# A matrix attention kernel: four products of two units take their operand blocks in reverse order

## The chip, the core and the metric

The kernel runs on one NeuronCore of a Trainium2 chip. The metric is the device time of one execution in microseconds (us). Before the change it was run five times: median 2456.31 us, from 2454.04 to 2456.42.

## What is computed

For each of four images x (64 x 64 positions, 256 channels), three projections are made, then an attention over the N = 4096 positions of the flattened image, then a scaled residual:

```python
q = jnp.einsum('bwhc,cd->bwhd', x, Wq) + bq
k = jnp.einsum('bwhc,cd->bwhd', x, Wk) + bk
v = jnp.einsum('bwhc,cd->bwhd', x, Wv) + bv
pq = q.reshape(B, -1, N)
pk = k.reshape(B, -1, N)
pv = v.reshape(B, -1, N)
energy = jnp.einsum('bcn,bcm->bnm', pq, pk)
attention = jax.nn.softmax(energy, axis=-1)
out = jnp.einsum('bcm,bnm->bcn', pv, attention)
return gamma * out + x
```

pq and pk have 128 rows (channels), pv has 256. The softmax runs over m, the 4096 positions of k and v.

## The kernel before, in words

**Stages.** The images follow each other. For each, sixteen projection steps (lines 493 to 505) transpose x and make q, k and v; then 128 steps, `for u in range(STEPS)` (line 507), do the attention. A *group* g is 256 of the 4096 columns n; there are 16 groups. A group is worked through in eight *units* t = 0 to 7, `g, t = divmod(u, NU)`; a unit is 512 of the 4096 positions m, in four blocks of 128.

**Precision.** The matmuls of the attention are of type fp32r. Each operand is held as an upper part h, a remainder l, and a form d that mixes both with a small factor E; three products put the result together: h with `vh`, l with `vl` (both added up in `acc`), and d with `vd` (added up in `bb`). The three forms of v lie in SBUF for the whole image: `vh` and `vl` have rows of VC = 260 floats (256 channels, a column of ones for the softmax's sum, and padding; lines 220 and 221), `vd` rows of 256 floats (line 222). The h, l and d of a unit are tiles of 4 x 256 floats in rotating buffers (three for h, two each for l and d).

**One step u.** It issues, in this order: the energies of unit u + 3 in two halves (`energy`, lines 317 to 339; six matmuls each, of 256 columns, into `sa` and `sb`, with an exponential of each on ACT); between the halves, the product x*y on DVE and the upper part h on ACT for unit u + 2 (`join`, line 344, `upper`, line 349); a load of the k tile for unit u + 5 (line 314, on POOL's queue); l and d of unit u + 1 on DVE (`halves`, lines 355 and 358); and the products of unit u (`attend`, line 380). When a group ends, its result is copied out of PSUM and finished during the first steps of the next group (`finish`, lines 400 to 422); this puts four transposes (line 417) on PE, behind the products of t = 1. In the first group of an image there are none. In the last three steps of an image there are no more energies. On PE, then, behind the products of a unit t stand the energies that the next step issues.

**The order on PE** is written out by hand (`tc.manual_schedule()`): no scheduler moves it. In `attend` there are 24 matmuls for a unit: for h, then l, then d; in each for j = 0, 1 (the two halves of 128 columns n, `NJ` = 2), and in each of these over i = 0 to 3, the four blocks of m. The block number is 2t, 2t + 16, 2t + 1, 2t + 17 for i = 0, 1, 2, 3. The weights of a product are a block of 128 x 128 of h, l or d; the moving operand is a row block of vh, vl (258 columns) or vd (256 columns). All four products of one (form, j) add up in the same place of PSUM. Line 378 has the block number, line 377 the loop over i, and line 382 the addresses' step, `left[:, i, j * P : (j + 1) * P]`.

Of the kernel before, what the change touches and what calls it, by code (L numbers as in the profile page):

```python
# [20 lines left out]
def kernel(  # L21
# [154 lines left out]
    NJ = NB // P  # L176
# [24 lines left out]
    with ExitStack() as fast:  # L201
# [161 lines left out]
        def attend(b, u):  # L363

            g, t = divmod(u, NU)
            if t == 0:
                now["acc"] = [
                    ps_o.tile([P, C + 2], F32, tag=f"a{j}", name=f"a{j}_{b}_{g}")
                    for j in range(NJ)
                ]  # L370
                now["bb"] = ps_o.tile([P, NJ, C], F32, tag="bb", name=f"bb_{b}_{g}")
            h, l, d = units[b, u]
            acc, bb = now["acc"], now["bb"]
            for left, right in ((h, vh), (l, vl), (d, vd)):
                for j in range(NJ):
                    out_ = bb[:, j, :] if left is d else acc[j]
                    for i in range(4):
                        m = 2 * t + i // 2 + NI * (i % 2)

                        nc.tensor.matmul(  # L380
                            out_,
                            left[:, i, j * P : (j + 1) * P],
                            right[:, m, : out_.shape[1]],
                            start=(t == i == 0 and (left is h or left is d and j == 0)),
                            stop=(t == NU - 1 and i == 3 and left is not h),
                            skip_group_check=True,
                        )
            if t == NU - 1 and (b, g) != (B - 1, NG - 1):
                o = now["o"] = work.tile([P, NJ, C + 2], F32, tag="o", name=f"o_{b}_{g}")
                for j in range(NJ):  # L390
                    nc.scalar.activation(o[:, j, :], acc[j], AF.Identity, scale=1.0 + E)
# [94 lines left out]
        for b in range(B):  # L486
# [20 lines left out]
            for u in range(STEPS):  # L507
                g, t = divmod(u, NU)
# [33 lines left out]
                for forms in beside:  # L542
                    next(forms)
                attend(b, u)
                if (b, u) == (B - 1, STEPS - 1):
                    finish_last(b, g, loads.pop((b, "x", g)))
# [11 lines left out]
    NJ = NB // P  # L558
# [131 lines left out]
```

## Time and profile before

One profiled execution took 2456.11 us as a run; the span from its first to its last instruction was 2454.3 us.

| what | value |
|---|---|
| median of five runs | 2456.31 us |
| profiled execution / its span | 2456.11 / 2454.3 us |
| mean granted TensorE clock | 0.998 |
| h products (line 380), 4096 matmuls of 258 columns | 574.4 us busy |
| l products, 4096 of 258 columns | 572.8 us busy |
| d products, 4096 of 256 columns | 558.6 us busy |
| energies (line 330), 4096 into sa, 2048 into sb | 735.6 and 567.0 us busy |
| longest wait of another engine for PE: POOL for sb before a load of k | 1547.1 us in 428 waits |
| DMA, mean | 203 GB/s |

How to read it: "PE" is the matmuls, "PEld" the loading of their weights, which runs beside them. A matmul's duration in a row (279 to 283 ns) is not the time between two of them: they are pipelined, and the end of each is modelled. The time that a stretch of matmuls takes is read from starts: the start of the first matmul behind the stretch minus the start of its first. Consecutive matmuls of the same line and tiles stand in one row of the timeline, with their number (x8).

Lines 199 and 124 in a row of PE are the warm-up transposes and the transposes of x at the start; line 460 is the last output's transposes at the end.

### The profile page before, as it was taken

To read this page: it belongs to the slowest core of one execution; us is meant where nothing else is said; L and a number is where in the kernel's file an instruction comes from. 1 tells how busy PE (TensorE), PEld (TensorE's weight loads), DVE (VectorE), ACT (ScalarE), POOL (GpSimd) and SP (SyncE) were. 2 spreads that over 40 slices of the span, in tenths; PEclk is the share of its full clock that TensorE was granted. 3 is DMA by queue.
4 is the path that set the end of the run, shared out by engine and by line. 5 is a ranking of instruction groups with operands and counts; after the bars stand their busy time and mean duration, and the time that the engine had idled before them with its cause. 6 is when DMAs were issued, how large, how long until landed. Compare 5 with 4: busy or idle time off the path is not lost.

```text
span 2454.3 us, 50024 instructions
## 1 busy us (share of the span) xinstructions
PE 2440.5 (99%) x19982; PEld 2409.2 (98%) x19982; DVE 2099.6 (86%) x2314; ACT 1796.9 (73%) x3201; POOL 425.8 (17%) x781
## 2 busy tenths in 40 slices
PE   9999999999999999999999999999999999999998
PEld 8999999999899999999989999999998999999998
DVE  5988888888698888888869888888886988888887
ACT  5877777777677777777667777777766777777775
POOL 4211111111411111111141111111114111111110
PEclk9999999999999999999999999999999999999999
DMA  7666666665776666666477666666647766666663
GB/s 230 214 209 203 209 206 199 209 207 159 226 224 200 206 211 203 205 201 207 150 240 224 200 201 210 203 208 202 205 142 245 228 203 198 207 205 212 202 202 112
DMA packets 137407, 498.92 MB, mean 203 GB/s; under 512 B 15536, under 2 KB 57264, under 8 KB 137168
## 3 DMA queue, kind: packets, MB, share of 16 engines
q0 software_dynamic: 92320, 453.17, 60.1%
q1 hardware_dynamic: 44304, 42.22, 5.6%
q8 instruction: 160, 2.62, 0.4%
q14 instruction: 79, 0.65, 0.1%
q10 hardware_dynamic: 544, 0.26, 0.0%
HBM read 445.25 MB, written 50.33 MB: 202 GB/s over the span
## 4 chain that ended last, share of the span: by engine, by line


## 5 line engine op out<-in xcount | busy, mean ns | idle before, releaser
L334 ACT ACTIVATE x<-sa 128x512 f32<-128x512 f32 x1024 | 613.7, 599 | 514.2 <-PE sa L330 512.0
L344 DVE TENSOR_TENSOR x<-x,y 128x1024 f32<-128x1024 f32 x512 | 626.9, 1224 | 233.9 <-ACT y L334 233.9
L330 PE MATMUL sa<-q,k 128*128 128x256 f32 x4096 | 735.6, 279 | 0.0
L355 DVE TENSOR_TENSOR l<-x,h 128x1024 fp32r<-128x1024 f32 x512 | 623.9, 1219 | 0.0
L358 DVE SCALAR_TENSOR_TENSOR d<-h,x 128x1024 fp32r<-128x1024 f32 x512 | 623.8, 1218 | 0.0
L330 PEld LDWEIGHTS sa<-q,k 128*128 128x128 f32 x4096 | 619.5, 188 | 0.5
L334 ACT ACTIVATE y<-sb 128x512 f32<-128x512 f32 x1024 | 615.2, 601 | 0.0
L380 PE MATMUL a<-vh,h 128*128 128x258 f32 x4096 | 574.4, 283 | 0.0
L380 PE MATMUL a<-vl,l 128*128 128x258 f32 x4096 | 572.8, 282 | 0.0
L330 PE MATMUL sb<-q,k 128*128 128x256 f32 x2048 | 567.0, 277 | 0.0
L380 PE MATMUL bb<-vd,d 128*128 128x256 f32 x4096 | 558.6, 279 | 0.0
L314 POOL DMA_DIRECT2D k<-kf x512 | 280.0, 547 | 1572.1 <-PE sb L330 1547.1
L349 ACT ACTIVATE h<-x 128x1024 fp32r<-128x1024 f32 x512 | 543.7, 1062 | 8.4 <-DVE x L344 7.9
L380 PEld LDWEIGHTS a<-vl,l 128*128 128x128 f32 x4096 | 525.3, 189 | 0.0
L380 PEld LDWEIGHTS a<-vh,h 128*128 128x128 f32 x4096 | 522.9, 189 | 0.0
L380 PEld LDWEIGHTS bb<-vd,d 128*128 128x128 f32 x4096 | 515.1, 188 | 0.0
L330 PEld LDWEIGHTS sb<-q,k 128*128 128x128 f32 x2048 | 384.5, 188 | 0.2 <-DVE q L266 0.2
L137 PE MATMUL qk<-wqk_sb,xts 128*128 128x256 f32 x512 | 122.4, 382 | 0.0
L158 PE MATMUL v<-xts,wv_sb 128*128 128x256 f32 x512 | 120.3, 379 | 0.0
L158 PEld LDWEIGHTS v<-xts,wv_sb 128*128 128x128 f32 x512 | 97.3, 190 | 13.2
L137 PEld LDWEIGHTS qk<-wqk_sb,xts 128*128 128x128 f32 x512 | 93.0, 191 | 10.3
L275 POOL DMA_DIRECT2D qd<-qks x128 | 69.4, 550 | 180.7 <-DVE qks L146 171.7
(56 smaller groups left out, 866.0 us busy)
## 6 DMA issues: line engine op xcount, KB each, us to landing
k<-kf POOLq DMA_DIRECT2D x512, 768.0 KB, 4.7
x<-in_x_dram SPq DMA_DIRECT2D x128, 256.0 KB, 3.9
kf<-f POOLq DMA_DIRECT2D x64, 384.0 KB, 3.9
out_dram<-x POOLq DMA_DIRECT2D x63, 256.0 KB, 2.6
qd<-qks POOLq DMA_DIRECT2D x128, 64.0 KB, 3.0
qr<-qd SPq DMA_DIRECT2D x64, 128.0 KB, 3.6
wv_sb<-in_L_conv_Wv_dram POOLq DMA_DIRECT2D x1, 256.0 KB, 7.3
out_dram<-x SPq DMA_DIRECT2D x1, 256.0 KB, 4.1
```

The lines of the kernel that those rows point to most:

```text
L137: nc.tensor.matmul(qk[:, s, :], self.xt[i][:, k, s, :], wqk_sb[:, k, :], start=(k == 0), stop=(k == KC - 1),)
L158: nc.tensor.matmul(vp[:, eh, :], wv_sb[:, k, eh * P : (eh + 1) * P], self.xt[i][:, k].rearrange("p s a -> p (s a)"), start=(k == 0), stop= ...
L275: nc.gpsimd.dma_start(qd[b, i // 2 + NG // 2 * s][:, i % 2, :], x[:, s, :C2])
L314: nc.gpsimd.dma_start(t.rearrange("p (i s) f d -> p i s (f d)", s=2), kf[b, u % NU])
L330: nc.tensor.matmul(to[:, i], kt[:, 2 * k + i, f, :], q[:, f], start=first, stop=last)
L334: nc.scalar.activation(to[:, 2 * k : 2 * k + 2, :], sp.rearrange("p i j d -> p i (j d)"), AF.Exp, scale=scale,)
L344: nc.vector.tensor_tensor(x, x, y, ALU.mult)
L349: nc.scalar.activation(h, units[b, u], AF.Identity, scale=UPPER)
L355: nc.vector.tensor_tensor(l, x, h.bitcast(F32), ALU.subtract)
L358: nc.vector.scalar_tensor_tensor(d, h.bitcast(F32), 1.0 + E, x, ALU.mult, ALU.subtract)
L380: nc.tensor.matmul(out_, left[:, i, j * P : (j + 1) * P], right[:, m, : out_.shape[1]], start=(t == i == 0 and (left is h or left is d and ...
```

## The change

In the units t = 1 and t = 3 of each group, the four l products for j = 1, the last four l products of the unit, run over i = 3, 2, 1, 0 in place of 0, 1, 2, 3. So the block numbers there are 2t + 17, 2t + 1, 2t + 16, 2t. All other products keep their order; each product keeps its own weights, its own rows of vl and its place in PSUM.

```diff
             for left, right in ((h, vh), (l, vl), (d, vd)):
                 for j in range(NJ):
                     out_ = bb[:, j, :] if left is d else acc[j]
-                    for i in range(4):
+                    back = left is l and j == NJ - 1 and t in (1, 3)
+                    for i in reversed(range(4)) if back else range(4):
                         m = 2 * t + i // 2 + NI * (i % 2)
```

The changed file has three more lines than the file before, so line 380 of before is line 383 of after.

## The prediction

> **What bounds the kernel now.** I read the page first (busy shares, clock), then PE's waits, then the groups by form, then the timeline of PE alone over one group, and last the start of every single matmul in the trace.
>
> ```profile
> span 2454.3 us, 50024 instructions
> PE 2440.5 (99%) x19982; PEld 2409.2 (98%) x19982; DVE 2099.6 (86%) x2314; ACT 1796.9 (73%) x3201; POOL 425.8 (17%) x781
> PEclk9999999999999999999999999999999999999999
> ```
>
> PE is busy from end to end at a granted clock of 0.998. Its own waits are three rows of 5.6 us in all, at the start and the very end:
>
> ```profile
> PE wp L199 <- POOL ident masks.py:199: 2.4, 1, 2.4
> PE xt L124 <- DMA x<-in_x_dram: 2.1, 1, 2.1
> PE ot L460 <- DVE o L455: 1.1, 1, 1.1
> ```
>
> So in between, the time is the number of matmuls times the pace at which they start, and nothing on DVE, ACT, POOL or the queues sets it. The pace is not one number. The timeline of PE for t=2 to t=4 of one group (start, length, engine, line; what counts is the start of the next row minus that of a row; the length has the modelled tail of the last matmul in it):
>
> ```profile
> 865.08 1.12 PE L380 MATMUL a<-vh,h 128*128 128x258 f32 x8
> 866.03 1.12 PE L380 MATMUL a<-vl,l 128*128 128x258 f32 x8
> 866.99 1.08 PE L380 MATMUL bb<-vd,d 128*128 128x256 f32 x8
> 867.90 0.39 PE L330 MATMUL sa<-q,k 128*128 128x256 f32 x2
> ...
> 869.26 1.11 PE L380 MATMUL a<-vh,h 128*128 128x258 f32 x8
> 870.21 1.12 PE L380 MATMUL a<-vl,l 128*128 128x258 f32 x8
> 871.17 1.11 PE L380 MATMUL bb<-vd,d 128*128 128x256 f32 x8
> 872.12 0.40 PE L330 MATMUL sa<-q,k 128*128 128x256 f32 x2
> ...
> 873.54 1.12 PE L380 MATMUL a<-vh,h 128*128 128x258 f32 x8
> 874.49 1.12 PE L380 MATMUL a<-vl,l 128*128 128x258 f32 x8
> 875.45 1.09 PE L380 MATMUL bb<-vd,d 128*128 128x256 f32 x8
> 876.38 0.39 PE L330 MATMUL sa<-q,k 128*128 128x256 f32 x2
> ```
>
> The eight d products take 0.91 us in t=2 and 0.95 in t=3; the twelve energy matmuls behind them (next h start minus first sa start) take 1.36 and 1.42. Same instructions, same forms, no wait. By single starts, the d products and energies settle at one of two paces: 113.3 ns (**short**), or a cycle of 117.5, 117.5 and 118.3 ns, mean 117.8 (**long**). Six of the eight units of a group (t=0, 2, 4, 5, 6, 7) settle short and two, t=1 and t=3, settle long; this repeats within a nanosecond in the groups of all four images. The h and l products never settle: they wander between 113 and 125 ns.
>
> The pace has a memory: in t=1 the transposes of the previous group's output come behind the d products, and the energies behind these run short again. In the first group of an image there are no such transposes, and the energies of t=1 stay long:
>
> ```profile
> 83.50 1.10 PE L380 MATMUL bb<-vd,d 128*128 128x256 f32 x8
> 84.44 0.40 PE L330 MATMUL sa<-q,k 128*128 128x256 f32 x2
> ...
> 85.85 1.12 PE L380 MATMUL a<-vh,h 128*128 128x258 f32 x8
> ```
>
> 85.85 minus 84.44 is 1.41. The pace also depends on addresses: rows of vh and vl are 260 floats, 1040 bytes, so each step of m moves the moving operand by 16 bytes against its weights (whose steps are 512), while vd's rows are 1024 bytes and keep one place. In t=1 all rounds of four but the first repeat 120.0, 120.9, 123.3, 115.8 ns over i, for h and for l. So: the last l products leave the PE's two reads in some relation, and the d products, all with one relation of addresses, fall from it into short or long and carry it through the energies until h begins.
>
> **The change, part by part.** The built program differs from before in the operands of 512 matmuls (4 images x 16 groups x 2 units x 4) and nowhere else: counts, waits and semaphore updates stand at the same places; l of a unit is read by the same eight matmuls and released by the last of them. No engine gets more or other work, and no queue is passed. What is left is pace.
>
> *Reordered products.* The four take 480.0 ns (t=1) and 475.9 (t=3) now. The same four in the other six units take 468 to 483, mean 476. Reversed they lie, by the nearest rows, between 12 ns less and 7 more; I take 476: 4 ns off in t=1, nothing in t=3, 64 x 4 = 0.3 us (ends: 1.3 off, 0.6 on).
>
> *d products of t=3.* 948 ns now; the six short units take 916 to 930, mean 923. If released, 25 ns off (18 to 32). *Energies of t=3:* 12 x (117.8 - 113.3) = 54 ns off. Together 79 (72 to 86), and all 64 groups have energies there: 64 x 79 = 5.1 us (4.6 to 5.5).
>
> *d products of t=1.* 944 ns, the last of them slowed by the transpose behind it; released, 923 plus 4 for that: 17 off (10 to 24), in 60 groups 1.0 us. In the four first groups the energies are long too: 4 x (19 + 54) = 0.3 us. Together 1.3 (0.9 to 1.7).
>
> *t=4 behind a short t=3.* It now starts from long energies, then from short ones. The nearest row is t=2, seen both ways: h, l and d take 2831 ns from long (first group), 2826 from short. 64 x 5 = 0.3 us off; with 8 ns to either side, from 0.2 on to 0.8 off.
>
> *Cover.* A unit of t=3 shortens from 4.28 us to about 4.20, which is what t=4 takes with the same work beside it: DVE's three passes of 1.2 us, ACT's exponentials (which wait for PE). k tiles land 4.7 us after issue and are loaded two units, over 8 us, ahead. l for t=4 is ready at 870.19 and first read at 874.49. Nothing is late next.
>
> Is the new entry short? The trace does not show it. By the row of v last read before d, t=0 to 7 end on m = 17, 19, 21, 23, 25, 27, 29, 31; 19 and 23 give long. The change ends on m=2 and m=6: even rows, which never come last now. The bounds are no release (0) and full release; I take release, since six of eight entries end short, from very different pasts, and t=2 ends short from both kinds of entry.
>
> [...]
>
> **The sum.** 5.1 + 1.3 + 0.3 + 0.3 = 7.0 us off. The profiled execution took 2456.11 us (its span 2454.3 and 1.8 around it) and would take 2449.1; the median of the runs is 2456.31, so 2449.3 us.
>
> **The rivals.** 0.2% is 4.9 us, about what a measurement of this kernel can tell from no change.
>
> - *Only t=3 is released:* 5.1 + 0.3 from t=4: 2450.9 us. For it: the two units enter from different rows (m=2, m=6), so they need not go together.
> - *Only t=1:* 1.3 + 0.3: 2454.7 us.
> [...]
> - *Slower: the long pace spreads.* t=3 stays long, leaves its energies in another place of the three-step cycle, and t=4 (short today, always entered from t=3's long energies) goes long too. Price: 60 groups x (25 + 54) and 4 last groups (no energies) x 25 = 4.8 us, and 0.6 more with the upper end of the four products: 2461.7 us. It decides from the point where more units go long than are freed. Against it: t=2 stays short from both entries.
>
> **How the numbers follow.** Both released 0.55 (2449.3, own range, with all ends added, 2447.0 to 2451.6); only t=3 0.14; only t=1 0.12; neither 0.13; spread 0.06. The range runs from the far end of the likeliest case, 2447.0, to the case of t=1 alone with the upper end of the four products, 2455.2, and leaves out 0.19. Faster by over 0.2%: 0.55 and most of the 0.14, since its sum of 5.4 is barely over 4.9, so 0.65; within 0.2%: the rest of it, t=1 alone and neither, 0.29; slower 0.06.
>
> **What would show it.** In the timeline of PE in the changed kernel: t=3 d products about 0.92 us and energies 1.36, the unit 4.20; t=1 d products 0.92; in an image's first group, energies of t=1 1.36. PE's waits stay the three rows. t=4 stays at 4.20 us; if it reads 4.28, the long pace has moved there. If t=3 still reads 1.42 for its energies, the entry did not release it, and the forecast is wrong; if the time falls but the energies don't, my account of where it sits is wrong.

## The result, and the profile after

The changed kernel takes 2450.24 us (median of 25 runs, 2448.47 to 2451.92); before took 2455.73 us (45 runs, 2453.18 to 2457.20). The ratio is 0.9979, with a 95% interval of 0.9974 to 0.9985: 5.5 us less, 0.21%. The forecast was 7.0 us less, 2449.3 us.

The page after, and PE's own waits in it: the same number of instructions, the same three waits, and PE 5.5 us less busy (2435.0 for 2440.5). The granted clock is 0.998 in both. The busy times of the other engines (DVE is VectorE, ACT ScalarE, POOL GpSimd) differ by 1.4 us at most.

```profile
span 2448.9 us, 50024 instructions
PE 2435.0 (99%) x19982; PEld 2403.4 (98%) x19982; DVE 2099.5 (86%) x2314; ACT 1795.5 (73%) x3201; POOL 424.5 (17%) x781
```

```profile
PE wp L199 <- POOL ident masks.py:199: 2.4, 1, 2.4
PE xt L124 <- DMA x<-in_x_dram: 2.1, 1, 2.1
PE ot L463 <- DVE o L458: 1.1, 1, 1.1
```

The timeline of PE after, for t=1 to t=3 of the group that the prediction showed (start, length, engine, line; differences of starts count):

```profile
860.34 1.10 PE L383 MATMUL bb<-vd,d 128*128 128x256 f32 x8
861.28 0.60 PE L420 MATMUL ot<-ident,o 128*128 128x128 f32 x4
861.64 0.48 PE L330 MATMUL sa<-q,k 128*128 128x256 f32 x2
...
863.13 1.11 PE L383 MATMUL a<-vh,h 128*128 128x258 f32 x8
864.09 1.12 PE L383 MATMUL a<-vl,l 128*128 128x258 f32 x8
865.04 1.08 PE L383 MATMUL bb<-vd,d 128*128 128x256 f32 x8
865.95 0.39 PE L330 MATMUL sa<-q,k 128*128 128x256 f32 x2
...
867.31 1.11 PE L383 MATMUL a<-vh,h 128*128 128x258 f32 x8
868.26 1.12 PE L383 MATMUL a<-vl,l 128*128 128x258 f32 x8
869.22 1.08 PE L383 MATMUL bb<-vd,d 128*128 128x256 f32 x8
870.14 0.39 PE L330 MATMUL sa<-q,k 128*128 128x256 f32 x2
...
871.50 0.88 PE L383 MATMUL a<-vh,h 128*128 128x258 f32 x6
```

In t=3 the d products now take 0.92 us (870.14 minus 869.22; before 0.95), and the energies behind them 1.36 (871.50, the next h start, minus 870.14; before 1.42): t=3 has gone to the short pace. In t=1 the transposes and the energies together, which the prediction left as they were, have grown: from the first sa to the next h is 1.49 us (863.13 minus 861.64). The same place before:

```profile
863.62 0.49 PE L330 MATMUL sa<-q,k 128*128 128x256 f32 x2
...
865.08 1.12 PE L380 MATMUL a<-vh,h 128*128 128x258 f32 x8
```

That is 1.46 us.

By single starts, with before and after taken unit by unit over all 64 groups:

| unit | ns a group | us in all | where |
|---|---|---|---|
| t=3 | -86 in every group | -5.49 | four products -3, d -29, energies -53 |
| t=1, first group of an image | -70 | -0.28 | products -8, d -8, energies -53 |
| t=1, groups with transposes | -13 in 32, +28 in 28 | +0.37 | products -8, d -5 to -9, transposes and energies +4 or +42 |
| t=2 | -8 in 28 groups, -4 in first groups | -0.25 | entered from long energies behind t=1; in first groups, from short ones |
| t=4 | -1 | -0.05 | |
| t=0, 5, 6, 7, with the stretches between images | | +0.30 | only in last groups and between images |

The sum is 5.4 us, the span fell by 5.5. Units that the change does not touch take the same in both profiles (t=5: 4.20 us), so a different clock is not the cause. Spans of single executions differ by up to 3 us more, because the first unit begins at a time of its own (75.1 to 78.4 us in the profiles here; 77.37 before and 77.31 after). For that reason the sums over units are compared below wherever they say more than the median.

### The profile page after: what moved, and what is told of

It is laid out like the page before. It is cut to its first block, busy times and chain, and to the rows that moved or that the text cites. A ratio compares the mean times of both kernels' runs of the same rounds, so it can differ in the third digit from the quotient of the medians.

```text
span 2448.9 us, 50024 instructions
## 1 busy us (share of the span) xinstructions
PE 2435.0 (99%) x19982; PEld 2403.4 (98%) x19982; DVE 2099.5 (86%) x2314; ACT 1795.5 (73%) x3201; POOL 424.5 (17%) x781
## 4 chain that ended last, share of the span: by engine, by line
## 5 line engine op out<-in xcount | busy, mean ns | idle before, releaser
L137 PEld LDWEIGHTS qk<-wqk_sb,xts 128*128 128x128 f32 x512 | 93.2, 192 | 10.4
```

The source lines that it names most:

```text
L137: nc.tensor.matmul(qk[:, s, :], self.xt[i][:, k, s, :], wqk_sb[:, k, :], start=(k == 0), stop=(k == KC - 1),)
```

## The experiments

### One half of the change each

Edits, against the changed kernel:

```diff
-                    back = left is l and j == NJ - 1 and t in (1, 3)
+                    back = left is l and j == NJ - 1 and t == 3                      # e1_t3_only
+                    back = left is l and j == NJ - 1 and t == 1                      # e2_t1_only
+                    back = left is l and j == NJ - 1 and (t == 3 or t == 1 and g == 0)  # e3_t1_first
```

> Only the unit t=3 of each group takes its last four l products in reverse order; t=1 runs as before. My theory (the order sets how the PE's two reads stand when d begins, and d and the energies keep it): all of the gain of the change is here: d of t=3 -29 ns, energies -53, the four products -3, 64 groups: 5.5 us less than before in the span (about 2448.8), the same time as the full change within 0.3 us. d products of t=1 back at 944 ns and energies behind its transposes short. Rival (each of the two units gives its share, as I had forecast): 1.3 us less gain than the sum of both, span about 2450.0. Rival (other engines: the unit is shorter because DMA or DVE traffic falls elsewhere): no clean split by unit.

Measured: 2449.99 us, ratio to before 0.9975 (0.9965 to 0.9985). Sum over units 5.3 us less: t=3 -5.49, t=4 -0.05, the others as before but for one unit t=0 that took 0.2 us more.

> Only t=1 is reversed; t=3 runs as before. My theory: almost nothing in sum. In the first group of each image 70 ns less (no transposes there), in the others 15 ns less in the products and 20 to 40 ns more in the energies behind the four transposes, 4 to 8 ns less in t=2: within 0.4 us of before. t=3 stays long (d 948, energies 1413 ns), since t=2 in between settles short from either entry. Rival (t=1's release is worth what I forecast): 1.3 us less. Rival (t=3's pace hangs on t=1): t=3 changes too, by up to 5 us.

Measured: 2454.33 us, ratio 0.9996 (0.9987 to 1.0005). Sum over units 0.05 us less: t=1 +0.09, t=2 -0.24, t=3 as before to the ns.

> t=3 reversed in every group, t=1 only in the first group of an image, where no transposes stand behind it. My theory: the 5.5 us of t=3 plus 4 x 70 ns = 0.3 us, span about 2448.5, 0.2 to 0.5 below the full change by the trace and not told from it by the runs. Rival (the energies of t=1 run long in the full change for another reason than what stands ahead of the transposes): they stay long here as well, in groups after the first.

Measured: 2449.09 us, ratio 0.9972 (0.9962 to 0.9983), not to be told from the full change by these intervals; sum over units 5.8 us less, 0.4 below the full change. Of the 5.8, t=1 gave 0.28 and t=3 5.49. In later groups t=1 is as before.

So the two halves are independent, and t=3 is the whole gain. t=1 gains where no transposes stand behind it and a little in 32 other groups, and loses that again in the remaining 28.

### All orders of the four products

```diff
-                    for i in reversed(range(4)) if back else range(4):
+                    order = range(4)
+                    if left is l and j == NJ - 1 and t in (1, 3):
+                        order = list(permutations(range(4)))[(NG * b + g) % 24]
+                    for i in order:
```

> The last four l products of t=1 and t=3 run over the 24 orders of i, one order for each group in turn (16 groups x 4 images, so each order two or three times), read by group in the trace. My theory (a state carried from product to product): the outcome is a fixed one for each order and unit; d and energies of t=3 settle at one of few paces, short (energies 1360 ns) in about three quarters of the orders and long (1413) in the rest, and the two known orders give what they gave before. Rival (the row of v that is read last decides): all six orders with the same last i give the same energies. Rival (reversal is special, or the gain is from elsewhere): most orders are long, or the same order differs from group to group by tens of ns. The span lies between 2447 and 2456.

The span was 2452.3 us. Read by group, t=3 repeats itself within 1 ns wherever an order comes again: twelve orders give short energies (1360 ns), twelve long (1413 to 1414). It is the row class (even or odd row of vl) of the last product that divides them: all twelve that end on i = 0 or 1 (rows 2t, 2t + 16) are short, all twelve that end on i = 2 or 3 (rows 2t + 1, 2t + 17) are long. i = 0 and 1 are 16 rows of 1040 bytes, 16640 bytes, apart, and so are i = 2 and 3; no run varies that distance. The rival "the row read last decides" describes t=3 as well as mine does; that three quarters would be short was wrong. In t=1 the outcome was not a fixed one for each order: in eight of the 24 orders the transposes and energies took 1810 to 1816 ns in one group and 1850 to 1854 in another. The timeline of PE for t=3, from d on, in two groups that follow each other, with order 2, 0, 1, 3 and order 2, 0, 3, 1:

```profile
502.10 1.11 PE L385 MATMUL bb<-vd,d 128*128 128x256 f32 x8
503.04 0.40 PE L330 MATMUL sa<-q,k 128*128 128x256 f32 x2
...
504.46 0.28 PE L385 MATMUL a<-vh,h 128*128 128x258 f32 x1
```

```profile
536.22 1.07 PE L385 MATMUL bb<-vd,d 128*128 128x256 f32 x8
537.13 0.39 PE L330 MATMUL sa<-q,k 128*128 128x256 f32 x2
...
538.49 0.28 PE L385 MATMUL a<-vh,h 128*128 128x258 f32 x1
```

One exchange of the last two products: d 0.94 and 0.91, energies 1.42 and 1.36 us. The second order also makes its four products 468 ns long, where the reversal of the change has 472.5 and the order of before 476.

### The same reversal in h

The edit is `left is h` for `left is l` in the line of `back`.

> In t=1 and t=3 the last four h products (j=1) run in reverse in place of the last four l products. My theory (the state is set by the last few products ahead of d, and forgotten over some eight): the eight l products behind, in the order of before, bring t=3 back to where it was: d 948, energies 1413 ns, t=1 d 944, span 2454.3 within 0.5 us. Rival (a reversal anywhere in the unit shakes it out of the long pace): t=3 energies 1360 and 5 us less.

Sum over units 1.7 us less (the span, 2450.6, fell by 3.7, of which the earlier start of the first unit is 2.0). t=3 came out as expected: d 948, energies 1413, only the products ahead of them 13 ns shorter. t=1 did not: its d products lost 22 to 26 ns, and in first groups the energies ran short (81.46, 82.37 and 83.73 for d, energies and the next h, 0.91 and 1.36 us). In odd groups from 3 on, transposes and energies took 1853 ns, as in the full change:

```profile
81.46 1.08 PE L383 MATMUL bb<-vd,d 128*128 128x256 f32 x8
82.37 0.39 PE L330 MATMUL sa<-q,k 128*128 128x256 f32 x2
...
83.73 0.28 PE L383 MATMUL a<-vh,h 128*128 128x258 f32 x1
```

Eight l products behind the reordering of h were enough for d and energies to be as before in t=3 (948 and 1413 ns), and not in t=1.

### Addresses alone

```diff
-        pool("pad", 1).tile([P, 16], F32, name="pad")
         ppool = pool("ppool", 2)
-        pool("pad2", 1).tile([P, 112], F32, name="pad2")
+        pool("pad2", 1).tile([P, 128], F32, name="pad2")
```

> The kernel before, with 64 bytes of padding moved from ahead of the buffers x, y, h, l, d to behind them: these lie 64 bytes lower, all other tiles, and so the energies' operands, stay. Order and work are those of before. My theory (how the two reads of PE stand to each other is an affair of addresses): h, l and d products change their paces, the d products no longer settle at 113.3 ns in six units (sum of eight moves by more than 10 ns in most units), while the energies keep their two paces. Rival (the pace comes from the order of issue or from other engines' and the DMAs' traffic): d stays at 914 to 948 ns in each unit and the span at 2454 us within 0.5.

2489.39 us against 2453.96 for before beside it; sum over units 35.4 us more, with the order of before, the same instructions, PE's three waits of 4.8 us in all, and DVE, ACT and POOL as busy as ever (2099.5, 1795.8 and 424.5 us):

```profile
span 2487.6 us, 50024 instructions
PE 2474.6 (99%) x19982; PEld 2443.7 (98%) x19982; DVE 2099.5 (84%) x2314; ACT 1795.8 (72%) x3201; POOL 424.5 (17%) x781
```

The d products no longer settle at 113.3 ns in any unit (most run between 116 and 121), and the energies, whose own operands have not moved, run long in all eight units: that is 21.6 of the 35.4 us, d gives 10.4, h and l together 3.2. The two paces are not the only ones: in t=1, t=2 and t=4 some d products in a row now run at 120.0 ns. The timeline of t=2, short before and after the change:

```profile
876.71 1.11 PE L379 MATMUL bb<-vd,d 128*128 128x256 f32 x8
877.66 0.40 PE L329 MATMUL sa<-q,k 128*128 128x256 f32 x2
...
879.08 0.28 PE L379 MATMUL a<-vh,h 128*128 128x258 f32 x1
```

d 0.95 and energies 1.42 us. With the order kept and 35.4 us more, the order of issue does not make the pace by itself: where the moved tiles lie has a part in it, and the energies, their own operands in place, ran 21.6 us longer behind slower d products. Only the weights' tiles moved here and the rows of v stayed, so whether it is the weights' own place that counts, or their place to the moving operand, is not separated. DVE and ACT write and read the moved tiles too. Against them and the DMAs as the cause speaks the last unit of the kernel before: from 2440.92 to 2442.85 us ACT and POOL do nothing there, DMA moves 0 GB/s and DVE makes one copy of 0.16 us. Yet each step between its h and l products is within 1 ns of the same step in a group with all engines at work (h 963 and l 964 ns, there 964 and 963).

### All orders in all units

```diff
-                    for i in range(4):
+                    order = range(4) if left is d else list(permutations(range(4)))[(NG * b + g) % 24]
+                    for n, i in enumerate(order):
...
-                            start=(t == i == 0 and (left is h or left is d and j == 0)),
-                            stop=(t == NU - 1 and i == 3 and left is not h),
+                            start=(t == n == 0 and (left is h or left is d and j == 0)),
+                            stop=(t == NU - 1 and n == 3 and left is not h),
```

> All four h and l loops of all eight units run over one of the 24 orders of i, one order for each group in turn. It asks whether the rule that the first table showed for t=3 (energies short when the last row of vl is 2t or 2t+16, long when it is 2t+1 or 2t+17) holds in every unit. By that rule read alone: orders that end on i = 0 or 1 give short energies (1360 ns) in all units. By my theory (a state carried from product to product, for which each unit has rows of its own): t=3 follows it again, while t = 0, 2, 4 to 7, which are short with odd last rows today, follow no single rule; orders that alternate between odd and even rows make the four products 5 to 10 ns shorter than 0, 1, 2, 3. The span lies between 2446 and 2462.

The span was 2458.7 us. t=3 follows the rule of the last row in all its groups again. No other unit does: t=0 is mostly the other way round (long when the last row is even), t=5 is long in four orders only (2, 0, 1, 3; 2, 1, 0, 3; 3, 0, 1, 2; 3, 1, 0, 2), t=4 in four others. So "the last row decides" falls as a rule, and what holds is that each unit has a fixed answer to each order when it is entered from short energies: within 2 ns, in groups of different images.

### The best order of each unit

```diff
+ORDERS = (
+    (1, 2, 0, 3), (0, 2, 1, 3), (0, 1, 2, 3), (2, 0, 3, 1),
+    (3, 2, 1, 0), (0, 2, 1, 3), (0, 2, 1, 3), (2, 0, 1, 3),
+)
...
+                    for n, i in enumerate(range(4) if left is d else ORDERS[t]):
```

(with `start` and `stop` as in the kernel before it.)

> For each of the eight units the order of i (for h and l, both j) that gave the shortest unit in the table by order: t=0: 1,2,0,3; t=1: 0,2,1,3; t=2: 0,1,2,3; t=3: 2,0,3,1; t=4: 3,2,1,0; t=5 and 6: 0,2,1,3; t=7: 2,0,1,3. My theory (a unit that is entered from short energies repeats itself to the ns, whatever came before): the gains of the table add up, 7, 20, 0, 99, 14, 0, 6 and 14 ns a group, 160 x 64 = 10.2 us less than before, span 2444.1, and 2443.6 to 2446 if t=1 behaves otherwise in the groups that the table did not show. Rival (the units hang together through more than the pace at which they are entered): single units go long, 85 ns a group each, and the span lies above 2448.

2445.77 us, ratio to before 0.9964 (0.995 to 0.9977). Sum over units 9.5 us less. t=0, 2, 3, 4, 6 and 7 gave what the table said (-7, 0, -99, -14, -6, -14 ns), t=0 13 more in first groups, and t=2 8 more where it is entered from long energies. t=1 gave its 20 in even groups and took 22 more than before in the odd ones from group 3 on, the case left open in the expectation. But for t=1 the gains of the table add up.

### What the transposes behind t=1 do

In the full change, t=1's energies behind the transposes take 1814 ns in even groups and in group 1, and 1853 in odd groups from 3 on. The transposes read one of two buffers o, in turn.

```diff
-        pool("pad3", 1).tile([P, 48], F32, name="pad3")
...
-                o = now["o"] = work.tile([P, NJ, C + 2], F32, tag="o", name=f"o_{b}_{g}")
+                o = now["o"] = work.tile([P, 2 * 288], F32, tag="o", name=f"o_{b}_{g}")[:, : NJ * (C + 2)].rearrange("p (j c) -> p j c", j=NJ)
...
```

(The o of the last group is changed alike; its line is left out.)

> The changed kernel with its two buffers o, which the transposes behind t=1 read, 2304 bytes apart in place of 2080, so that both lie alike to 256 bytes (the first stays where it is; the k tiles move by 256 bytes). In the changed kernel the energies behind these transposes are 1814 ns in even groups and group 1, and 1853 in odd groups from 3 on. Theory A (the address of o decides how the transposes are entered and left): the groups no longer alternate, all read 1814 or all 1853, and nothing else changes. Theory B (something else that alternates by group decides, since group 1 has the buffer of the odd groups and yet goes with the even ones): the pattern stays.

All groups with transposes read 1815 to 1817, and the sum over units is 0.9 us below the full change. For t=1 of an odd group, here and in the next run:

> The changed kernel with the k tiles 256 bytes further on, as in the run before, but with the buffers o where they were. In that run the alternation by group behind t=1 was gone, yet the odd groups read the buffer o that had stayed in place. Theory A (the address of k, which the energies behind the transposes read as weights, released them): the odd groups read 1815 here as well. Theory B (the other buffer o did it, by a way that this does not show): odd groups from 3 on read 1853 again.

(Its edit is 112 for 48 in the tile `pad3` of the changed kernel.) Here odd groups read 1853 again: the address of k is not it. The timeline of PE, first with the buffers o apart, then with k apart; from the first sa to the next h, 1.46 and 1.49 us:

```profile
860.66 0.49 PE L329 MATMUL sa<-q,k 128*128 128x256 f32 x2
...
862.12 0.28 PE L382 MATMUL a<-vh,h 128*128 128x258 f32 x1
```

```profile
861.70 0.48 PE L330 MATMUL sa<-q,k 128*128 128x256 f32 x2
...
863.19 0.28 PE L383 MATMUL a<-vh,h 128*128 128x258 f32 x1
```

So the place of the second buffer o (and of the small tile r behind it, which moved with it) takes the alternation away: 1815 to 1817 ns in all groups with transposes, in place of 1814 and 1853. But the odd groups read the first buffer, which has not moved. How the one acts on the other, and why group 1 goes with the even ones, stays open. Group 1 is the first in an image with transposes behind t=1; that something left by the transposes of earlier groups counts would fit both, but no run tests it.

### Both together

The kernel with the best orders and the buffers o apart, faster than both kernels:

> The kernel with the best order of each unit, and the buffers o 2304 bytes apart as in the run before last. If the release of t=1's odd groups holds with these orders too, 28 groups x 39 ns = 1.1 us less than the best orders alone in the sum of the units, 10.6 us less than before; the runs' median near 2445. If not, 9.5 us less than before.

2444.47 us, ratio to before 0.9953 (0.994 to 0.9967): 11.6 us less in the median; sum over units 10.6 us less, as expected, of it t=3 6.3 and t=1 1.5.

## Why the prediction was right, and where it was not

**What bounds the kernel** held: in the profiles of before, after, the padding and the buffers o apart PE waits at the ends alone, 4.6 to 5.6 us in all, and the time is the pace of its matmuls. Padding moved by 64 bytes, 35.4 us more in the sum over units, shows that the pace hangs on addresses; one exchange of two products, energies of t=3 at 1.42 or 1.36 us, that it hangs on order. The account of paces that are entered from the products ahead held for t=3, but the pace at entry is not the whole state. In first groups before, t=2 follows long energies and needs 2830 ns for h, l and d; in 28 groups after it follows long energies behind transposes and needs 2818. How addresses and order make a pace was not isolated: the prediction's "relation" of PE's two reads is the author's supposition, and no run shows it.

**The release of t=3** came, but its ground did not hold. The prediction took it because six of eight entries end short; of the 24 orders only twelve free t=3, and the rule that picks them there holds in no other unit. So the reversed order was as likely as not to free t=3, and that it did was in part luck. The size was right: d and energies, forecast as 79 ns a group (72 to 86), lost 82, energies 53 for 54 and d 29 for 25. That is 5.28 us for 5.1.

**The release of t=1 was the step that failed.** Forecast: 17 ns of d in 60 groups, 1.0 us, on the ground that the energies behind the transposes "run short again". d lost only 5 to 9 ns, and in 28 of the 60 groups the energies behind the transposes then ran long, 42 ns more. So the transposes did not clear the state: with another order ahead of them, the stretch behind them went from 1811 to 1853 ns in these groups, and that the energies ran short in all 60 groups before belonged to how the transposes were entered then. In the four first groups, without transposes, 73 ns were forecast, of them 19 for d, where the rows before give 15 (938 to 923). d lost 8 and the energies 53, 61 in all. In sum d and what stands behind it in t=1 cost 0.62 us more, where 1.3 less was forecast; with its four products t=1 gave +0.09 us.

**Smaller terms.** The four reversed products: 0.3 us forecast, 0.75 measured (8 ns in t=1, 3 in t=3, inside the bounds). t=4 behind short energies: 0.3 forecast, 0.05 measured; the row of t=2 was no good stand-in, and it gives 2830 and 2827 ns, 3 apart where the prediction has 5. Instead t=2, now entered from long energies in 28 groups, gave 0.25, which was nowhere in the sum; nor were the 0.30 us more in last groups and between images.

**The rivals.** What happened is nearest to "only t=3", 2450.9 us, which had a chance of 0.14; by pace both units were released, and it was the stretch behind t=1 that gave its gain back. Of the 7.0 us, 5.4 came: t=1 fell short by 1.9, and the other terms together gave 0.3 more than forecast. The time lies only 0.9 us from the forecast, because before itself was 0.6 us faster in its 45 runs than in the five that the forecast starts from. The spread of the long pace to t=4 did not come: t=4 stayed at 4.20 us. Nor did the case that neither unit is released, with its chance of 0.13: the energies of t=3 fell to 1.36 us.

## What to carry to other kernels

When PE never waits, read the starts of its matmuls: here equal instructions ran at paces 4% apart (113.3 and 117.8 ns), and the twelve energies of a unit kept the pace in which they were entered (1.36 or 1.41 us in t=3), so the place to change can lie ahead of the place that is slow. Where such an effect repeats to the ns, as here, one kernel can try a different order in each repetition of a loop and give a whole table; take each stretch's best entry from it and check the sum in one run. Before counting a gain, follow it through every matmul behind: in 28 groups t=1 gained 13 ns and lost 42 behind its four transposes.

## What the runs showed of the hardware that was not expected

- A move of the weights' tiles of the h, l and d products by 64 bytes, the moving operand staying, cost 35.4 us in the sum over units (1.4%), though PE waited for nothing between the start and the end, and no instruction changed.
- The paces repeat: over 56 groups of before (all but the first and last of each image) every start within a unit repeats within 1 ns, but within 4 behind the transposes of t=1.
- With all addresses kept, the order alone sets how long the four l products of t=3 take: 476 ns for 0, 1, 2, 3 and 467 or 468 for 2, 0, 3, 1, which alternates between the two row classes.
